# Pace of dispatch scatters, held result scatters and order of first statistics in a gated-recurrence and top-2 MoE kernel

## The chip, the cores and the metric

The kernel runs on one core of a Trainium2 chip. The metric is the device time of one execution in microseconds (us). A core has five engines with in-order queues: PE (matrix multiplication), DVE (vector), ACT (scalar), POOL (GpSimd) and SP (which here only issues DMAs). POOL issues the scatters, that is, indirect DMAs whose rows go to addresses read from a tile.

## The reference, cut to what matters

Input x is 32 sequences of 256 tokens of 128 floats (8192 tokens). For each sequence a modulation from c gives shifts, scales and gates. Then:

```
h   = layernorm(x) * (1 + scale_a) + shift_a
a   = sigmoid(h Wd + bd);  v = h Wv + bv;  g = sigmoid(h Wg + bg)
hs_t = a_t * hs_{t-1} + (1 - a_t) * v_t        (scan over the sequence)
x1  = x + gate_a * hs * g
h2  = layernorm(x1) * (1 + scale_b) + shift_b
p   = softmax(h2 gate_w^T + gate_b) over 8 experts; the two largest are kept
moe = sum over these two of p[e] * (relu(h2 w1[e] + b1[e]) w2[e] + b2[e])
out = x1 + gate_b * moe                        (|gate_a|, |gate_b| at least 0.25)
```

Each expert has w1 of 128x512 and w2 of 512x128, all in fp32.

## The kernel before, in words

**First phase.** The tokens are worked on in 16 supertiles s = 0 to 15 of 512 tokens (T = 4 tiles of 128). A supertile has four steps: `a_norm` (L328: first statistics on DVE by `stats` L292 and `rsqrt` L300, normalised rows xn on ACT), `a_mix` (L349: px transposes, three pz products, the scan on DVE), `a_res` (L385: po transposes, residual, second statistics, rows xm), `a_route` (L401: ph transposes, logits pl, pb transposes, rows `rw` L418, top 2, ranks by the product pq L439, destination rows `pi` L456, and rw's two further columns: weight L461 and the token's result row L462).

**Dispatch.** rw has 8 pieces of 128 rows per supertile. `send` (L472) scatters one by pi into `reg`, a DRAM array that holds the rows of each expert together. The 8 scatters go into the list `sending`; `drip` (L487) takes 1 or 2 of it after each step and gives each a wait on `behind`, an ACT instruction of the step just written: a pace. 128 such scatters run in all.

**Tables and blocks.** After the supertiles of `TAKE` and after the last one, `table` (L497) computes on DVE which blocks of 256 rows of `reg` are full. Blocks 0 to 4 come from supertile 2's table, blocks up to 44 from those up to supertile 12, blocks 45 to 70 from the last. A table's blocks are released when the last scatter of its supertile has been issued.

**Second phase.** A block has four steps: `b_load` (L559, SP: its rows xr and its expert's weights ww; it waits for the latest 16 dispatch scatters), `b_in` (L573: pbx transposes, xs on ACT and DVE), `b_up` (L583: products p, hidden rows hh), `b_down` (L604: products pby, rows yt on ACT, then two result scatters L617 on POOL, yd<-yt). The row index of a result scatter is read from a column of xr. `b_step` (L679) does one step of each of three consecutive blocks and loads four ahead. While the first phase runs, `between` (L710) puts a `b_step` after most of its steps if over two blocks are ready.

**Sums.** `c_base` (L624) adds the experts' biases to xa; `c_load` (L650) reads the two result rows of each token from yd into yk; `c_add` (L660) writes the output. They need constants of `late_constants` (L231), which is called after part 9 of the list of steps.

**What sets the order.** Each engine works in order. The order is that of a list scheduler over the program's own order, with priorities: steps of the first phase from supertile 3 on are moved ahead by `AHEAD`. The first parts are written out in `HEAD` (L31). A tile whose buffers are all in use makes its writer wait: rw has 3 buffers, xr 14, yt 8, yk 3.

Of the kernel before, what the change touches and what calls it, by code (L numbers as in the profile page):

```python
# [8 lines left out]
F32 = mybir.dt.float32  # L9
F32R = mybir.dt.float32r  # L10
BF16 = mybir.dt.bfloat16
I32 = mybir.dt.int32
U32 = mybir.dt.uint32
AF = mybir.ActivationFunctionType
ALU = mybir.AluOpType
AX = mybir.AxisListType
WAIT = mybir.DependencyInfo(mybir.DependencyClass.Sync, mybir.DependencyReason.DATA)

P = 128
# [5 lines left out]
T = 4  # L25
# [4 lines left out]

HEAD = "n0|m0 n1|r0 m1 n2|R0 r1 m2 n3|R1 r2 m3 n4|R2 r3 m4 n5"  # L31

LATE = 9

XE = 3
EARLY = 3
PW = 3
# [3 lines left out]
BACK = 2  # L41
SKIP = 8

HA = 53


YTB = 8
CLAG = 3
HALF = 15

# [4 lines left out]
def adaln_moe(ctx: ExitStack, tc: tile.TileContext, x, Wg, bg, Wv, bv, Wd, bd,  # L55
              gate_w, gate_b, w1, b1, w2, b2, c, wmod, out):
    nc = tc.nc
    NB, S, D = x.shape
    E, _, H = w1.shape
# [3 lines left out]
    NS = N // ST  # L63
    BPS = ST // S
    JB = T // BPS
    K = 2
    CAP = N + BLK
    NJ = BLK // P
    RW = D + 2

    xf = x.rearrange("b s d -> (b s) d")
    of = out.rearrange("b s d -> (b s) d")
# [3 lines left out]
    wk = ctx.enter_context(tc.tile_pool(name="wk", bufs=2))  # L76
    bk = ctx.enter_context(tc.tile_pool(name="bk", bufs=3))
# [18 lines left out]
    xa = cp.tile([P, NS, T, D], F32, name="xa")  # L96
# [7 lines left out]
    rows = cp.tile([P, D], F32, name="rows")  # L104
# [56 lines left out]
    dst = cp.tile([P, NS * T, K], I32, name="dst")  # L161
# [107 lines left out]
    yd = dp.tile([K * N, D], F32, name="yd")  # L269
# [19 lines left out]
    mh = cp.tile([P, T, 1], F32, name="mh")  # L289
    nc.vector.memset(mh, -0.5)  # L290

    def stats(mv, src, name):  # L292
        n = src.shape[1]
        st = wk.tile([P, T, 6], F32, tag=f"st{name[0]}", name=f"st{name}")
        for j in range(n):
            nc.vector.bn_stats(st[:, j], src[:, j])  # L296
        for j in range(n):
            nc.vector.bn_aggr(mv[:, j], st[:, j])

    def rsqrt(mv, name, s):  # L300
# [22 lines left out]
        nc.vector.scalar_tensor_tensor(r, mv[:, :, 0:1], -1.0, y, op0=ALU.mult, op1=ALU.mult)  # L323
        return y, r

    ln1 = {}

    def a_norm(s):  # L328
        g = LN1G.get(s, 0)
        if g:  # L330
            mv = wk.tile([P, g * T, 2], F32, tag=f"mva{g}", name=f"mva{s}")
            for i in range(g):
                stats(mv[:, i * T:(i + 1) * T], xa[:, s + i], f"a{s + i}")
            y, r = rsqrt(mv, f"a{s}", s)
            for i in range(g):
                ln1[s + i] = (y[:, i * T:(i + 1) * T], r[:, i * T:(i + 1) * T])
        y, r = ln1[s]
        xn = wk.tile([P, T, D], F32, tag="xn", name=f"xn{s}")
        for j in range(T):
            last = nc.scalar.activation(xn[:, j], xa[:, s, j], AF.Identity, scale=y[:, j], bias=r[:, j])  # L340
        return dict(s=s, xn=xn, last=last)
# [59 lines left out]
    def a_route(a, base):  # L401
        s, xn = a["s"], a["xn"]
# [50 lines left out]
        pf = wk.tile([P, T, K], F32, tag="pf", name=f"pf{s}")  # L453
        nc.vector.tensor_reduce(pf, op_, axis=AX.X, op=ALU.add)
        pi = wk.tile([P, T * K], I32, tag="pi", name=f"pi{s}", bufs=3)
        nc.vector.tensor_copy(pi, pf.rearrange("p t k -> p (t k)"))  # L456
        sm = wk.tile([P, T], F32, tag="sm", name=f"sm{s}")
        nc.vector.tensor_reduce(sm, e8, axis=AX.X, op=ALU.add)
        rc = wk.tile([P, T], F32, tag="rc", name=f"rc{s}")
        nc.vector.reciprocal(rc, sm)  # L460
        nc.vector.tensor_tensor(rw[:, :, :, D], e8[:, :, 0:K], rc.unsqueeze(2).to_broadcast([P, T, K]), op=ALU.mult)  # L461
        nc.gpsimd.tensor_copy(rw[:, :, :, D + 1].bitcast(I32), dst[:, s * T:(s + 1) * T])  # L462
        nc.vector.tensor_tensor(oh, oh, rw[:, :, :, D].unsqueeze(3).to_broadcast([P, T, K, E]), op=ALU.mult)
        dg = wk.tile([P, T, E], F32, tag="dg", name=f"dg{s}")
        nc.vector.tensor_tensor(dg, oh[:, :, 0], oh[:, :, 1], op=ALU.add)
# [21 lines left out]
    def drip(n, behind):  # L487
        for _ in range(min(n, len(sending))):
            s, send, j, k = sending.pop(0)
            w = send(j, k)  # L490
            tc.add_manual_dep(w, behind.ins.name, WAIT, reason="pace of the rows on their way out")
            sent.append(w)
            if not sending or sending[0][0] != s:
                while held and held[0][0] <= s:
                    blocks.extend(held.pop(0)[1])
# [63 lines left out]
    def b_load(n, tb, i):  # L559
        with tc.issue_after(loaded[-1].ins) if loaded else nullcontext():  # L560
            e = nc.sync.value_load(tb[i:i + 1, 0:1], min_val=0, max_val=E - 1)
            r = nc.sync.value_load(tb[i:i + 1, 1:2], min_val=0, max_val=E * CAP)
        xr = bk.tile([P, NJ, RW], F32, tag="xr", name=f"xr{n}", bufs=YTB + 6)
        w = nc.sync.dma_start(xr, reg[bass.ds(r, BLK)].rearrange("(p t) d -> p t d", p=P))
        tc.add_to_no_dep_group("rows", w.ins)
        for x in sent[-2 * K * T:]:
            tc.add_manual_dep(w.ins, x.name, WAIT, reason="its rows")
        ww = bk.tile([P, WW], F32, tag="ww", name=f"ww{n}", bufs=5)
        b = dict(n=n, xr=xr, ww=ww, tb=tb, i=i)
        loaded.append(nc.sync.dma_start(ww, wd[bass.ds(e, 1)].rearrange("o p f -> p (o f)")))  # L570
        return b

    def b_in(b):  # L573
        n, xr = b["n"], b["xr"]
        px = psb.tile([P, 512], F32, tag="pbx", name=f"pbx{n}")[:, :BLK]
        for j in range(NJ):
            nc.tensor.transpose(px[:, j * P:(j + 1) * P], xr[:, j, 0:D], ident)  # L577
        xs = bk.tile([P, 2, BLK], F32R, tag="xs", name=f"xs{n}")
        nc.scalar.activation(xs[:, 0], px, AF.Copy)  # L579
        nc.vector.tensor_tensor(xs[:, 1], px, xs[:, 0], op=ALU.subtract)  # L580
        b["xs"] = xs

    def b_up(b):  # L583
        n, xs, ww = b["n"], b["xs"], b["ww"]
# [17 lines left out]
        b["hh"] = hh  # L602

    def b_down(b):  # L604
        n, xr, hh, i = b["n"], b["xr"], b["hh"], b["i"]
        py = psb.tile([P, 512], F32, tag="pby", name=f"pby{n}", bufs=2)[:, :NJ * D]
        e = nc.tensor.value_load(b["tb"][i:i + 1, 0:1], min_val=0, max_val=E - 1)
        we = wr[:, bass.ds(e, 1), :].rearrange("p o f -> p (o f)")
        for j in range(NJ):
            for k in range(NH):  # L610
                nc.tensor.matmul(py[:, j * D:(j + 1) * D], hh[:, k, j * P:(j + 1) * P], we[:, k * D:(k + 1) * D],  # L611
                                 start=(j == 0 and k == 0), stop=(j == NJ - 1 and k == NH - 1))
        yt = bk.tile([P, NJ, D], F32, tag="yt", name=f"yt{n}", bufs=YTB)
        for j in range(NJ):
            nc.scalar.activation(yt[:, j], py[:, j * D:(j + 1) * D], AF.Copy, scale=xr[:, j, D:D + 1])  # L615
        for j in range(NJ):
            w = nc.gpsimd.indirect_dma_start(  # L617
                out=yd, out_offset=bass.IndirectOffsetOnAxis(ap=xr[:, j, D + 1:D + 2].bitcast(I32), axis=0),
                in_=yt[:, j], in_offset=None, bounds_check=K * N - 1, oob_is_err=False)
            for g in ("yscat", "yrows"):  # L620
                tc.declare_no_dep(w.ins, group=g, reason="rows of other pairs")
            tc.add_to_no_dep_group("yscat", w.ins)

    def c_base(s):  # L624

# [22 lines left out]
            nc.vector.tensor_tensor(t[:, jq], t[:, jq], g[:, q].unsqueeze(1).to_broadcast([P, JB, D]), op=ALU.mult)  # L648

    def c_load(s):  # L650
        yk = wk.tile([P, K, T, D], F32, tag="yk", name=f"yk{s}", bufs=3)
        step = JB if s >= HALF else T
        for j0 in range(0, T, step):
            for k in range(K):
                r = k * N + s * ST + j0 * P
                w = nc.sync.dma_start(tiles(yk[:, k, j0:j0 + step]), tokens(yd, r, step * P))
                tc.add_to_no_dep_group("yrows", w.ins)
        return s, yk, step
# [20 lines left out]
    def b_step():  # L679

        nonlocal nload
        nonlocal based
        i = len(flow)
        while nload < len(blocks) and nload < i + 1 + LOOK:
            tb, q, ends = blocks[nload]
            blocks[nload] = b_load(nload, tb, q)
            blocks[nload]["ends"] = ends
            nload += 1
        b = blocks[i] if i < len(blocks) else None
        flow.append(b)  # L690
        if b:
            b_in(b)
        if i >= 1 and flow[i - 1]:
            b_up(flow[i - 1])
            drip(1 if alive else 2, flow[i - 1]["last"])
        if i >= 2 and flow[i - 2]:
            b_down(flow[i - 2])
            ended.extend(flow[i - 2]["ends"])
        if not alive and based < NS:
            c_base(based)  # L700
            based += 1
        if len(adding) >= CLAG or (adding and not ended and i >= len(blocks)):
            c_add(*adding.pop(0))
        if ended:
            adding.append(c_load(ended.pop(0)))

    slot = 0
# [2 lines left out]
    def between():  # L710
        nonlocal slot
        slot += 1
        if slot % SKIP and len(blocks) - len(flow) > BACK:
            b_step()

    counts = []
    st = {}
# [16 lines left out]
    for t, todo in enumerate(steps):  # L734
# [37 lines left out]

        for i, s in todo:
            (step0, step1, step2, step3)[i](s)
            drip(2 if t < len(steps) - NS or len(sending) > K * T else 1, st[s]["last"])
            between()
        if t == 0:
            for e in range(E):
                stage(e)
            late()  # L780
        if t == LATE:
            late_constants()
    alive = False
    while len(flow) < len(blocks) + 2 or ended or adding:
        b_step()
    assert not sending and not held


_INS = ['L0_attn_x', 'L0_attn_Wg', 'L0_attn_bg', 'L0_attn_Wv', 'L0_attn_bv', 'L0_attn_Wd', 'L0_attn_bd',
# [25 lines left out]
```

## Time and profile before

| | us |
|---|---|
| median of 12 runs | 468.2 (465.03 to 470.26) |
| the profiled execution | 464.82 |
| its span, first to last instruction | 463.1 |
| busy PE, DVE, ACT, POOL | 380.1, 318.0, 301.2, 293.2 |
| 128 dispatch scatters, L473 | 125.2 busy, 978 ns each |
| 142 result scatters, L617 | 143.3 busy, 1009 ns each |
| block 0 begins (first pbx) | 101.90 |
| block 45 begins | 347.40 |
| block 70 begins | 441.09 |

A line of the timeline reads: start, length, engine, line of the kernel, operation, out<-in by the program's names, how many, and in brackets the idle time of that engine just before with what ended it. "issue" is idle time for which the profile shows no wait. In the slices the span is cut into 40 parts of 11.6 us; each digit is an engine's busy share in tenths. In the table of windows each engine's busy us is followed by its number of instructions.

### The profile page before, as it was taken

How to read it: one execution, taken by the hardware profiler on the slowest of the kernel's cores; microseconds unless marked ns; L12 is line 12 of the kernel's file. 1: busy time of each engine (PE TensorE's matmuls, PEld its weight loads, DVE VectorE, ACT ScalarE, POOL GpSimd, SP SyncE). 2: the span in 40 equal slices, each digit the busy share in tenths (PEclk: the TensorE clock that was granted, in tenths of full speed). 3: DMA queues.
4: the chain of work that ended last, by engine and by line, in shares of the span. 5: the costliest groups of instructions: out<-in, count | busy, mean ns of one | idle time of the engine just before them, and what ended most of it. 6: DMA issues, size and time to landing. Idle time of an engine off the chain costs nothing.

```text
span 463.1 us, 11442 instructions
## 1 busy us (share of the span) xinstructions
PE 380.1 (82%) x2803; PEld 332.9 (72%) x2803; DVE 318.0 (69%) x1638; ACT 301.2 (65%) x742; POOL 293.2 (63%) x322
## 2 busy tenths in 40 slices
PE   3827467659999999996899869999838999989980
PEld 3315243438898899895898859899837999889980
DVE  7997999979889888784579634766425320464484
ACT  3857366577986998893687635767524667667750
POOL 4633655354777777777777777777774555546651
PEclk9975777778999999999799988999996999999996
DMA  6996211037736484555563765887429977999994
GB/s 199 366 339 213 83 35 35 29 102 243 224 112 185 150 234 151 170 164 168 167 181 97 226 188 154 236 245 206 121 65 282 280 236 239 303 342 332 325 341 142
DMA packets 55413, 91.57 MB, mean 198 GB/s; under 512 B 8654, under 2 KB 39964, under 8 KB 55350
## 3 DMA queue, kind: packets, MB, share of 16 engines
q1 hardware_dynamic: 46624, 73.89, 53.0%
q0 software_dynamic: 8672, 16.94, 10.5%
q8 instruction: 25, 0.41, 0.4%
q14 instruction: 38, 0.31, 0.2%
q10 hardware_dynamic: 54, 0.02, 0.0%
HBM read 64.30 MB, written 27.43 MB: 198 GB/s over the span
## 4 chain that ended last, share of the span: by engine, by line
PE 50%; DMA 21%; DVE 13%; issue 6%; ACT 5%; POOL 4%; SPq 1%; POOLq 0%; ACTq 0%; DVEq 0%
PE pby L611 18%; PE pz L362 7%; DMA yd<-yt,xr 7%; DMA reg<-rw,pi 6%; PE p L592 5%; PE p L593 5%; PE p L594 5%; DMA yk<-yd 4%; PE pbx L577 3%; DMA ww<-wd 2%; DMA xr<-reg 2%; POOL reg L473 2%; DVE sta L296 2%; PE px L353 2%; PE po L390 1%
## 5 line engine op out<-in xcount | busy, mean ns | idle before, releaser
L617 POOL DMA_INDIRECT yd<-yt,xr x142 | 143.3, 1009 | 72.9 <-ACT yt L615 32.4
L473 POOL DMA_INDIRECT reg<-rw,pi x128 | 125.2, 978 | 61.5 <-issue 23.8
L611 PE MATMUL pby<-wr,hh 128*128 x1136 | 160.8, 279 | 0.6 <-ACT hh L600 0.5
L611 PEld LDWEIGHTS pby<-wr,hh 128*128 128x128 f32 x1136 | 145.3, 194 | 6.7 <-issue 4.1
L600 ACT ACTIVATE hh<-p,ww 128x256 f32<-128x256 f32 x231 | 98.9, 474 | 33.7 <-PE p L594 25.4
L592 PE MATMUL p<-xs,ww 128*128 128x256 f32 x284 | 91.1, 322 | 0.4 <-issue 0.4
L593 PE MATMUL p<-xs,ww 128*128 128x256 f32 x284 | 81.1, 286 | 0.0
L594 PE MATMUL p<-xs,ww 128*128 128x256 f32 x284 | 81.0, 285 | 0.0
L615 ACT ACTIVATE yt<-pby,xr 128x128 f32<-128x128 f32 x142 | 44.6, 369 | 25.5 <-PE pby L611 25.4
L362 PE MATMUL pz<-h,wT 128*128 128x512 f32 x96 | 56.6, 710 | 5.4 <-ACT tg L377 2.9
L592 PEld LDWEIGHTS p<-xs,ww 128*128 128x128 f32 x284 | 54.7, 193 | 2.4 <-issue 1.9
L593 PEld LDWEIGHTS p<-xs,ww 128*128 128x128 f32 x284 | 55.0, 194 | 0.5 <-issue 0.5
L594 PEld LDWEIGHTS p<-xs,ww 128*128 128x128 f32 x284 | 54.6, 192 | 0.0
L580 DVE TENSOR_TENSOR xs<-pbx,xs 128x256 fp32r<-128x256 f32 x71 | 29.6, 417 | 25.6 <-ACT xs L579 25.6
L577 PE MATMUL pbx<-ident,xr 128*128 128x128 f32 x142 | 28.6, 283 | 14.9 <-DMA xr<-reg 12.8
L362 PEld LDWEIGHTS pz<-h,wT 128*128 128x128 f32 x96 | 19.6, 233 | 24.7 <-issue 11.3
L579 ACT ACTIVATE xs<-pbx 128x256 fp32r<-128x256 f32 x71 | 27.8, 392 | 13.4 <-PE pbx L577 13.3
L598 DVE TENSOR_SCALAR hh<-p,ww 128x256 f32<-128x256 f32 x53 | 25.4, 479 | 15.2 <-ACT hh L600 14.8
L340 ACT ACTIVATE xn<-xa,nra,nya 128x128 f32<-128x128 f32 x64 | 26.5, 494 | 10.9 <-DVE nra L323 10.9
L398 ACT ACTIVATE xm<-xa,nrb,nyb 128x128 f32<-128x128 f32 x64 | 26.5, 484 | 10.1 <-DVE nrb L323 10.0
L665 DVE TENSOR_TENSOR ot<-yk 128x512 f32<-128x512 f32 (+1 forms) x17 | 11.2, 660 | 30.9 <-DMA yk<-yd 30.1
L418 ACT ACTIVATE rw<-pb 128x1024 f32<-128x1024 f32 x16 | 16.4, 1025 | 23.8 <-DMA reg<-rw,pi 19.9
(191 smaller groups left out, 636.0 us busy)
## 6 DMA issues: line engine op xcount, KB each, us to landing
ww<-wd SPq DMA_DIRECT2D x71, 514.0 KB
xr<-reg SPq DMA_DIRECT2D x71, 130.0 KB
yk<-yd SPq DMA_DIRECT2D x30, 256.0 KB
wd<-wh SPq DMA_DIRECT2D x8, 514.0 KB
xa<-in_L_attn_x_dram SPq DMA_DIRECT2D x16, 256.0 KB
out_dram<-ot SPq DMA_DIRECT2D x15, 256.0 KB
yd<-yt,xr POOLq DMA_INDIRECT x142
w1s<-in_L_ffn_w_dram SPq DMA_DIRECT2D x8, 256.0 KB
```

The lines of the kernel that those rows point to most:

```text
L362: nc.tensor.matmul(z, wT[:, i], h1, start=True, stop=True)
L473: w = nc.gpsimd.indirect_dma_start(out=reg, out_offset=bass.IndirectOffsetOnAxis(ap=pi[:, j * K + k:j * K + k + 1], axis=0), in_=rw[:, j, ...
L577: nc.tensor.transpose(px[:, j * P:(j + 1) * P], xr[:, j, 0:D], ident)
L579: nc.scalar.activation(xs[:, 0], px, AF.Copy)
L580: nc.vector.tensor_tensor(xs[:, 1], px, xs[:, 0], op=ALU.subtract)
L592: nc.tensor.matmul(z, hi, xs[:, 0], start=True, stop=False)
L593: nc.tensor.matmul(z, hi, xs[:, 1], start=False, stop=False)
L594: nc.tensor.matmul(z, lo, xs[:, 0], start=False, stop=True)
L600: w = nc.scalar.activation(hh[:, k], p1[:, k - k0], AF.Relu, bias=bias)
L611: nc.tensor.matmul(py[:, j * D:(j + 1) * D], hh[:, k, j * P:(j + 1) * P], we[:, k * D:(k + 1) * D], start=(j == 0 and k == 0), stop=(j == ...
L615: nc.scalar.activation(yt[:, j], py[:, j * D:(j + 1) * D], AF.Copy, scale=xr[:, j, D:D + 1])
L617: w = nc.gpsimd.indirect_dma_start(out=yd, out_offset=bass.IndirectOffsetOnAxis(ap=xr[:, j, D + 1:D + 2].bitcast(I32), axis=0), in_=yt[:, ...
```

## The change

1. **Results wait.** `b_down` no longer issues its two result scatters; it puts them in the list `results`. `results_out`, called by `b_step`, issues them, oldest first and ordered behind the latest dispatch scatter. While dispatch goes on it leaves up to 8 blocks' scatters in the list (up to block 8 all, from there fewer, none from about block 24 to 28, then again up to 8); afterwards it issues 3 per block, and all before a `c_load`. For this yt has 16 buffers, xr 9 instead of 14, and a DVE copy keeps each block's row indices in a tile of its own, xi. yk takes the buffers of rw.
2. **No pace at first.** `drip` gives the scatters of supertiles 0 to 2 no wait, and issues all 8 after the routing step. Later, once the first phase is written, it takes 3 per block instead of 2. `between` starts with the step given by `FIRST`.
3. **First statistics stay back.** The `bn_stats` of `a_norm` are ordered, without a wait, behind the pi of the supertile routed last in the program's order.
4. The copy of `dst` into rw moves from POOL to DVE.
5. `late_constants` is called after all steps.

```
-LATE = 9
+FIRST = (6, 1)
-YTB = 8
+HOLD0 = 28
+HOLD = 8
+XRB = 9
+YTB = 8 + HOLD
...
-            nc.vector.bn_stats(st[:, j], src[:, j])
+            w = nc.vector.bn_stats(st[:, j], src[:, j])
+            if behind:
+                tc.add_manual_dep(w.ins, behind.name, ORDER, reason="not ahead of the supertiles that route")
...
-                stats(mv[:, i * T:(i + 1) * T], xa[:, s + i], f"a{s + i}")
+                stats(mv[:, i * T:(i + 1) * T], xa[:, s + i], f"a{s + i}", placed[-1] if placed else None)
...
-        nc.gpsimd.tensor_copy(rw[:, :, :, D + 1].bitcast(I32), dst[:, s * T:(s + 1) * T])
+        nc.vector.tensor_copy(rw[:, :, :, D + 1].bitcast(I32), dst[:, s * T:(s + 1) * T])
...
-            tc.add_manual_dep(w, behind.ins.name, WAIT, reason="pace of the rows on their way out")
+            if s >= EARLY:
+                tc.add_manual_dep(w, behind.ins.name, WAIT, reason="pace of the rows on their way out")
...
-        xr = bk.tile([P, NJ, RW], F32, tag="xr", name=f"xr{n}", bufs=YTB + 6)
+        xr = bk.tile([P, NJ, RW], F32, tag="xr", name=f"xr{n}", bufs=XRB)
...
+        xi = bk.tile([P, NJ], I32, tag="xi", name=f"xi{n}", bufs=YTB + 3)
+        nc.vector.tensor_copy(xi, xr[:, :, D + 1].bitcast(I32))
+        b["xi"] = xi
...
-        for j in range(NJ):
+        def send(j):
             w = nc.gpsimd.indirect_dma_start(
-                out=yd, out_offset=bass.IndirectOffsetOnAxis(ap=xr[:, j, D + 1:D + 2].bitcast(I32), axis=0),
+                out=yd, out_offset=bass.IndirectOffsetOnAxis(ap=xi[:, j:j + 1], axis=0),
                 in_=yt[:, j], in_offset=None, bounds_check=K * N - 1, oob_is_err=False)
...
+        results.extend((send, j) for j in range(NJ))
+    results = []
+    def results_out(most, left=0):
+        for _ in range(min(most, len(results) - left)):
+            send, j = results.pop(0)
+            with tc.issue_after(sent[-1]):
+                send(j)
...
-        yk = wk.tile([P, K, T, D], F32, tag="yk", name=f"yk{s}", bufs=3)
+        yk = wk.tile([P, T, K, RW], F32, tag="rw", name=f"yk{s}", bufs=3)
+        yk = yk.rearrange("p t k r -> p (t k r)")[:, :K * T * D].rearrange("p (k t d) -> p k t d", k=K, t=T)
...
-            drip(1 if alive else 2, flow[i - 1]["last"])
+            drip(1 if alive else 3, flow[i - 1]["last"])
...
+        if alive or sending:
+            results_out(K * T, NJ * min(max(HOLD - max(i - HOLD, 0) // 2, i - HOLD0, 0), HOLD))
+        else:
+            results_out(NJ + 1)
...
         if ended:
+            results_out(len(results))
             adding.append(c_load(ended.pop(0)))
...
-            drip(2 if t < len(steps) - NS or len(sending) > K * T else 1, st[s]["last"])
-            between()
+            drip(K * T if i == 3 and s < EARLY else 2 if t < len(steps) - NS or len(sending) > K * T else 1, st[s]["last"])
+            if (t, i) >= FIRST:
+                between()
...
-        if t == LATE:
-            late_constants()
+    late_constants()
```

More of the change, by code (lines that the diff above doesn't have):

```diff
@@ L16 @@
 AX = mybir.AxisListType
+ORDER = mybir.DependencyInfo(mybir.DependencyClass.NoSync, mybir.DependencyReason.DATA)
 WAIT = mybir.DependencyInfo(mybir.DependencyClass.Sync, mybir.DependencyReason.DATA)
@@ L290, in adaln_moe, with stats @@
     nc.vector.memset(mh, -0.5)
-    def stats(mv, src, name):
+    def stats(mv, src, name, behind=None):
         n = src.shape[1]
@@ L324, in rsqrt @@
         return y, r
+    placed = []
     ln1 = {}
@@ L455, in a_route @@
         pi = wk.tile([P, T * K], I32, tag="pi", name=f"pi{s}", bufs=3)
-        nc.vector.tensor_copy(pi, pf.rearrange("p t k -> p (t k)"))
+        placed.append(nc.vector.tensor_copy(pi, pf.rearrange("p t k -> p (t k)")).ins)
         sm = wk.tile([P, T], F32, tag="sm", name=f"sm{s}")
@@ L604, in b_down @@
     def b_down(b):
-        n, xr, hh, i = b["n"], b["xr"], b["hh"], b["i"]
+        n, xr, hh, i, xi = b["n"], b["xr"], b["hh"], b["i"], b["xi"]
         py = psb.tile([P, 512], F32, tag="pby", name=f"pby{n}", bufs=2)[:, :NJ * D]
@@ L785, in adaln_moe @@
         b_step()
-    assert not sending and not held
+    assert not sending and not held and not results
 _INS = ['L0_attn_x', 'L0_attn_Wg', 'L0_attn_bg', 'L0_attn_Wv', 'L0_attn_bv', 'L0_attn_Wd', 'L0_attn_bd',
```

## Prediction

> **What bounds the kernel now.** I read four views in this order: the page's slices (which engine is full when), the chain that ended last, a table of busy time by stage (columns: window, its length, then busy us with counts for PE, PEld, DVE, ACT, POOL, then the granted clock, DMA share and GB/s), and single instructions at the seams.
>
> ```profile
> PE   3827467659999999996899869999838999989980
> DVE  7997999979889888784579634766425320464484
> POOL 4633655354777777777777777777774555546651
> ```
> ```profile
> PE 50%; DMA 21%; DVE 13%; issue 6%; ACT 5%; POOL 4%; SPq 1%; POOLq 0%; ACTq 0%; DVEq 0%
> PE pby L611 18%; PE pz L362 7%; DMA yd<-yt,xr 7%; DMA reg<-rw,pi 6%; PE p L592 5%; PE p L593 5%; PE p L594 5%; DMA yk<-yd 4%; PE pbx L577 3%; DMA ww<-wd 2%; DMA xr<-reg 2%; POOL reg L473 2%; DVE sta L296 2%; PE px L353 2%; PE po L390 1%
> ```
> PE is full from slice 10 on, except in slices 18 to 28 here and there and at slice 29; up to slice 9 it is half idle while DVE is full. Half the chain is PE, but 13% of it are the two kinds of scatter, which POOL issues.
>
> ```profile
> 45.00:102.00 57.00, 35.11 (x136) 19.44 (x135) 53.90 (x369) 32.54 (x69) 31.96 (x34) 0.77 0.15 48
> 102.00:120.00 18.00, 17.16 (x125) 14.58 (x126) 14.88 (x105) 14.22 (x36) 8.16 (x11) 0.87 0.75 219
> 120.00:200.00 80.00, 79.53 (x630) 71.58 (x630) 69.10 (x394) 69.12 (x177) 61.99 (x66) 1.00 0.60 182
> 200.00:288.00 88.00, 75.76 (x592) 69.84 (x592) 55.95 (x321) 56.36 (x143) 67.86 (x73) 0.92 0.57 165
> 330.00:352.00 22.00, 12.81 (x93) 11.13 (x94) 8.23 (x21) 7.33 (x18) 16.82 (x18) 0.86 0.41 126
> ```
> ```profile
> 101.90 0.69 PE L577 MATMUL pbx<-ident,xr 128*128 128x128 f32 x2 [2.45 <-DMA xr<-reg]
> ...
> 347.40 0.69 PE L577 MATMUL pbx<-ident,xr 128*128 128x128 f32 x2 [7.01 <-DMA xr<-reg]
> ```
> The first is block 0, the second block 45, the first that needs the last table. Block 44 began at 330.09; blocks there are 3.9 us apart, so 347.40 − 330.09 − 3.9 = **13.4 us** of the span are a stall. It ends 3.5 us after POOL's last dispatch scatter:
>
> ```profile
> 74.23 0.96 POOL L473 DMA_INDIRECT reg<-rw,pi  x1 [3.12 <-ACT xn L340]
> ...
> 86.66 0.97 POOL L473 DMA_INDIRECT reg<-rw,pi  x1 [3.08 <-ACT rw L418]
> ...
> 94.16 0.96 POOL L473 DMA_INDIRECT reg<-rw,pi  x1 [5.27 <-ACT xm L398]
> ...
> 342.95 0.96 POOL L473 DMA_INDIRECT reg<-rw,pi  x1 [0.30 <-DMA yd<-yt,xr]
> ```
> The upper three are scatters of supertiles 0 to 2 that wait for the pace, not for data: such waits spread 24 of them over 45 to 95 us, and block 0 needs the 24th, the one at 94.16.
>
> So I split the span at three pbx starts: **stage 1** to block 0, 101.9; **stage 2** to block 36 (297.4), 195.5; **stage 3** to block 70 (441.1), 143.7; **end** 22.0; together 463.1. Around the span lie 1.7 us (464.8 for that execution), and the median of the runs, 468.2, lies 3.4 above it.
>
> **Part 1, no pace for the first 24 scatters, first statistics held back.** A scatter takes 0.96 us and the next follows 0.30 later, 1.27 together. Supertile 1's destinations (pi) are written at 58.96, supertile 2's at 67.95. Ahead of these DVE also did first statistics (64 × 277 + 64 × 153 ns, with the chain behind them 2.2 us a supertile) of some eight supertiles, 17 us, that no block needs yet. They go behind. Of it I take 2 us as gain for supertile 1's pi, because the path to pi runs through ACT and PE as well; bounds 0 and 8. From there POOL issues 16 scatters one behind the other (supertile 2's pi is there before the ninth), 16 × 1.27 = 20.3; 2.8 for landing and 2.2 for the load, as of the first blocks before: 58.96 − 2 + 20.3 + 5 = **82 us** (76 to 90; the upper end if supertile 2's nyb, a POOL operation that now stands behind supertile 0's eight scatters and two weight operations of 1.27, comes late by 8). Gain 20 in stage 1.
>
> Most of it is work that only moves. In the order of PE's instructions block 0 now stands 2.5 px, 2 pz, 2 po, 2 ph/pl/pb and 1 pq groups earlier. At the 120–200 rates (per supertile px 0.6, pz 2.9, po 0.6, ph, pl and pb 2.2, pq 0.4) that is 1.6 + 5.8 + 1.3 + 4.4 + 0.4 = 13.4 us more PE in stage 2. PE's work there was 17.16 + 79.53 + 75.76 and 8.5 up to block 36: 181.0 in 195.5 us, a share of 92.6%. Now 194.4; at that share **210 us**. Below: PE never waiting, 197. Above: DVE. It had 146.5; to it come nine supertiles' statistics, 20, some 1.75 supertiles of routing and mixing at 11.8 (the lines L292 to L471 had 59 us in 120–200, for five supertiles), 20.7, the copies of part 3, 7.5: 195. At the 86% that DVE reached in 120–200 these take 226. I take 210: PE's own share already holds 12 us idle in 200–288, and DVE would stand at 93%, as in 45–102 (53.9 of 57).
>
> **Part 2, results wait.** Up to 16 result scatters stay behind dispatch scatters. In POOL's order the last dispatch scatter is the 190th instead of the 210th. POOL runs without pause from 117 us on, with 41 done there, 169 more in 226.5 us, 1.34 each. After: 40 are due by about 115 too (24 without pace, two supertiles); so the 190th ends near 343 − 20 × 1.3 = 317, and block 45 can start at 320.5. PE reaches block 45 at 82 + 210 + 32.7 (block 36 to 44 before) + 3.9 = 328.6. The stall is gone with 8 us to spare: **stage 3** 143.7 − 13.4 = 130.3. If POOL is later by more than 8 us, each further one costs one. The held scatters come later, at 3 per block, where POOL is half idle (46.68 busy of 89 us in 352–441); so I cost them at nothing, and at most 8 × 1.3 = 10 if they reached the end.
>
> **Part 3, copies.** 71 int copies of 128×2 on DVE; nearest row the 128×8 cast L456, 209 ns, small chain operations 155: I take 0.15 each, 36 in stage 2, 5.4; 12 of the 16 dst copies 2 us (POOL's 243 ns are their price there); both in the sum of part 1. In stage 3 DVE is at 40%, nothing. The xr buffers fall from 14 to 9; with four blocks loaded ahead and three in work eight are in use: nothing, at most a load's 2.2 us at a few blocks.
>
> These DVE copies also meet POOL's descriptor work. Scatters beside DVE work took 0.96 in the middle, 1.36 at most. The Trainium skill, "SBUF — State Buffer", section "SBUF: two separate sides", says that DVE and GpSimd share a port pair which one instruction holds alone, and that an fp32 copy inside SBUF on VectorE keeps GpSimd from writing descriptors. By that rule 87 more copies could cost POOL an estimated 87 × 0.15 = 13 us, which would eat the margin and give 454 in place of 449. The trace shows scatters near their minimum among hundreds of DVE instructions, so I don't add it.
>
> **Part 4, late constants.** Thirteen small DVE operations (3.2 us, 135 to 141 before), eight loads on SP and a POOL memset (0.5) go to the last routing; on SP the loads keep their place in the order, so nothing is queued behind them that was not before. DVE is freer there (26 of 42 us in 288–330): nothing, at most 3.2. yk in rw's buffers: first needed when dispatch is over: nothing.
>
> **Sum.** 82 + 210 + 130.3 + 22 = 444.3, with 1.7 around it 446.0 against 464.8, −18.8; against the median 468.2 that is **449**.
>
> **Rivals.**
> *DVE bounds stage 2.* For: 195 us of work, and its order is fixed with the xi copies ahead of earlier blocks' work. Against: DVE ran at 95% in 45–102. At 226: 82 + 226 + 130.3 + 22 + 1.7 + 3.4 = 465; I give it 458 to 468.
> *Slower: the xi copy of a table's first block stops DVE.* In DVE's order the copy of block 29 stands right behind supertile 11's pi, that of 37 behind supertile 14's, that of 45 behind 15's and ahead of block 44's xs. Each waits for a load that waits for the last scatter of supertile 10, 12 or 15; routing, xs and hh stand behind it. In the new order supertile 10's last is the 134th scatter: 60 by 133 us and 74 × 1.34 later, 232; DVE comes there at 215 to 221. So 11 to 17 us; some of that is the idle time already in PE's share (ACT waited 6.55 and 6.66 for buffers of the same scatters). It decides from 19 us beyond it, over 6 a place; at 12 a place 36 − 19 = 17 over: 485.
> *No gain.* The 20 us of stage 1 are given back (PE idles in stage 2 as long, the last dispatch scatter is as late): 466 to 470.
> *More.* Both full engines without loss and block 0 at 76: 76 + 197 + 130.3 + 22 + 5.1 = 430.
>
> **How the numbers follow.** Forecast (440 to 458) 0.55, DVE 0.18, slower 0.12, no gain 0.08, more 0.07. Under 0.5%, 2.3 us, this kernel's runs can't tell from no change: faster (below 465.9) 0.55 + 0.07 + two thirds of DVE's, 0.12, = 0.74; same 0.08 + 0.06 = 0.14; slower 0.12. The range leaves out the slower case, half of "more" and the top of "no gain": 435 to 468.
>
> **What would show it.** Block 0's pbx at 76 to 90, and supertiles 0 to 2's scatters 1.27 apart from their pi on; if it starts later, the pace was not what held them. Block 36 near 292 with PE at 92% between; DVE over 95% there, or DVE idle before xi waiting for xr, names the first two rivals. Last dispatch scatter near 317, and pbx of block 45 without a wait of several us for xr. Scatters still near 0.97 us. The prediction fails if stage 2 takes over 225 us.

## The result and the profile after

The changed kernel takes 488.2 us (median of 15 runs, 484.69 to 490.53), the kernel before 467.9 (62 runs): ratio **1.0435**, 95% interval 1.0416 to 1.0454. Its profiled execution took 489.51 us, its span is 487.8. By the four stages of the prediction, in us:

| | before | forecast | after |
|---|---|---|---|
| stage 1, to block 0 | 101.9 | 82 | 81.7 |
| stage 2, to block 36 | 195.5 | 210 | 239.2 |
| stage 3, to block 70 | 143.7 | 130.3 | 144.5 |
| end | 22.0 | 22 | 22.5 |

Block 0 starts where it was forecast. All of the miss is in stages 2 (+29) and 3 (+14). PE is busy 206.2 of the 239.2 us of stage 2 (86%); the forecast had 194.4 of 210 (92.6%). The slices of the changed kernel (12.2 us each now):

```profile
PE   4754662997698799889888796998989999699980
DVE  7868893789886698756774676676746631445584
POOL 3737653015514577777777777457777777466561
```
PE is below 9 in most slices from 10 to 27, where before it was near 9. POOL shows 0, 1, 5, 5, 1 from slice 7 on, then 7s. A scatter is busy 0.97 us and the next starts 0.30 later, so **7 is a full POOL**: 0.97 of 1.27.

Next the table of windows, first of the kernel before, then of the changed one (POOL is the fifth busy time with its number of instructions). The bounds are events: a stretch begins or ends with the last dispatch scatter of supertile 5 (149 and 153) or 11 (263 and 294); 77 is that of supertile 2 in the changed kernel, and 117.40 is the first result scatter of the kernel before.

```profile
117.40:149.00 31.60, 31.60 (x254) 28.63 (x254) 28.72 (x166) 26.40 (x68) 24.43 (x26) 1.00 0.56 171
149.00:263.00 114.00, 105.89 (x829) 96.15 (x828) 85.79 (x478) 88.43 (x223) 88.06 (x95) 0.97 0.58 169
```
```profile
77.00:103.60 26.60, 20.18 (x133) 17.41 (x134) 13.98 (x74) 17.70 (x43) 0.96 (x1) 0.75 0.42 130
103.60:153.00 49.40, 39.52 (x239) 30.39 (x239) 43.63 (x327) 33.32 (x77) 22.81 (x24) 0.83 0.32 98
153.00:294.00 141.00, 124.73 (x914) 109.76 (x914) 98.29 (x603) 97.03 (x242) 101.99 (x102) 0.96 0.53 157
```
Before, POOL issues 88 scatters (48 of dispatch, 40 of results) in the 114 us between supertiles 5 and 11: 88 × 1.30 = 114, and between two of its instructions there is no gap above the usual 0.30. So POOL is full in this stretch, while PE is busy 105.89 of the 114 us. After, 24 scatters leave in the 49.4 us before 153, where there was room for 38, and none of them is a result. The results held there come out behind: 48 + 54 in the next 141 us (12 fewer results than before ahead of this stretch, 14 more in it, 22 fewer between it and the last dispatch scatter: 62 instead of 82 in all). The last dispatch scatter starts at 354.78 instead of 342.95.

The gap after supertile 2's scatters, and block 5, in the timeline of the changed kernel:

```profile
101.22 0.18 PE L448 MATMUL pq<-mk,tri 128*128 128x40 bf16 x1
...
103.62 0.96 POOL L482 DMA_INDIRECT reg<-rw,pi  x1 [25.44 <-ACT hh L614]
...
132.53 0.69 PE L587 MATMUL pbx<-ident,xr 128*128 128x128 f32 x2 [2.93 <-DMA xr<-reg]
```
Blocks 0 to 4 now stand ahead of supertile 3 on PE, so its rank product comes at 101.22 (89.66 before), POOL idles for 25 us, and block 5 waits until 132.53. A later pause of POOL shows where the held-back statistics act:

```profile
152.65 0.96 POOL L482 DMA_INDIRECT reg<-rw,pi  x1 [0.30 <-ACT hh L614]
158.76 1.26 ACT L349 ACTIVATE xn<-xa,nra,nya 128x128 f32<-128x128 f32 x3 [2.82 <-DVE nra L330]
160.95 0.95 POOL L482 DMA_INDIRECT reg<-rw,pi  x1 [7.34 <-ACT xn L349]
```
The scatter at 160.95 is the first of supertile 6, whose pi is written at 147.78. It waits for its pace, an xn of a later supertile, and that xn waits for nra, the end of a chain that begins with first statistics at 147.86, right behind that pi.

Two more stalls are new, in stage 3, both on SP's in-order queue:

```profile
328.00 7.34 SPq L563 DMA_DIRECT2D reg<-pad  x7
...
336.99 0.35 SPq L574 DMA_DIRECT2D xr<-reg  x1
...
340.46 0.44 PE L587 MATMUL pbx<-ident,xr 128*128 128x128 f32 x2 [1.93 <-DMA xr<-reg]
```
```profile
414.72 0.93 SPq L684 DMA_DIRECT2D yk<-yd  x2
416.99 0.36 SPq L574 DMA_DIRECT2D xr<-reg  x1
418.51 0.69 DVE L693 TENSOR_TENSOR ot<-yk 128x512 f32<-128x512 f32 x1 [8.09 <-DMA yk<-yd]
...
419.59 0.69 PE L587 MATMUL pbx<-ident,xr 128*128 128x128 f32 x2 [4.17 <-DVE xs L590]
```
First block 39, 12.0 us after block 38: its load stands behind the pad writes of the last table. Before, such writes (292.60 to 301.03) held a load back as well, to 301.87, but PE had blocks enough and began one every 4 us. Then a yk load that waits 6.2 us for result scatters, with the loads of the next blocks behind it on SP: block 58 begins 8.0 us after block 57, where 3.4 is usual there. The stall ahead of block 45 did shrink as forecast: 366.33 − 359.00 = 7.3 us after block 44, without a wait for xr, instead of 17.3. So in stage 3 the shorter stall and the new ones cancel: 144.5 us against 143.7.

### The profile page after: what moved, and what is told of

Same layout as the page of the kernel before. It is cut to its first block, busy times and chain, and to the rows that moved or that the text cites. A ratio compares the mean times of both kernels' runs of the same rounds, so it can differ in the third digit from the quotient of the medians.

```text
span 487.8 us, 11431 instructions
## 1 busy us (share of the span) xinstructions
PE 393.7 (81%) x2803; PEld 341.3 (70%) x2803; DVE 323.4 (66%) x1725; ACT 303.4 (62%) x742; POOL 293.5 (60%) x306
## 4 chain that ended last, share of the span: by engine, by line
PE 27%; DMA 23%; DVE 10%; issue 10%; POOL 6%; ACT 5%; SPq 4%; POOLq 1%; ACTq 0%; DVEq 0%
PE pby L625 11%; DMA reg<-rw,pi 8%; DMA xr<-reg 7%; POOL reg L482 4%; PE p L606 4%; PE p L607 3%; PE p L608 3%; DMA yd<-yt,xi 2%; DMA yk<-yd 2%; DMA ww<-wd 2%; PE pbx L587 2%; POOL yd L632 2%; PE pz L371 1%; ACT xn L349 1%; ACT xm L407 1%
## 5 line engine op out<-in xcount | busy, mean ns | idle before, releaser
L632 POOL DMA_INDIRECT yd<-yt,xi x142 | 146.2, 1030 | 58.8 <-issue 22.2
L606 PE MATMUL p<-xs,ww 128*128 128x256 f32 x284 | 94.0, 333 | 4.6 <-DMA ww<-wd 2.0
L607 PE MATMUL p<-xs,ww 128*128 128x256 f32 x284 | 83.4, 294 | 0.0
L608 PE MATMUL p<-xs,ww 128*128 128x256 f32 x284 | 82.6, 291 | 0.0
L594 DVE COPY xi<-xr 128x2 int32<-128x2 int32 x71 | 14.3, 202 | 87.9 <-DMA xr<-reg 85.1
L606 PEld LDWEIGHTS p<-xs,ww 128*128 128x128 f32 x284 | 56.6, 200 | 9.6 <-DVE hh L612 2.7
L371 PE MATMUL pz<-h,wT 128*128 128x512 f32 x96 | 60.2, 749 | 3.2 <-ACT h L366 1.1
L607 PEld LDWEIGHTS p<-xs,ww 128*128 128x128 f32 x284 | 57.2, 201 | 0.7 <-issue 0.7
L608 PEld LDWEIGHTS p<-xs,ww 128*128 128x128 f32 x284 | 56.7, 200 | 0.1
L587 PE MATMUL pbx<-ident,xr 128*128 128x128 f32 x142 | 29.6, 292 | 22.2 <-DVE xs L590 11.8
L587 PEld LDWEIGHTS pbx<-ident,xr 128*128 128x128 f32 x142 | 17.5, 147 | 27.4 <-DVE xs L590 13.4
L371 PEld LDWEIGHTS pz<-h,wT 128*128 128x128 f32 x96 | 20.7, 246 | 20.5 <-issue 12.9
```

The source lines that it names most:

```text
L371: nc.tensor.matmul(z, wT[:, i], h1, start=True, stop=True)
L606: nc.tensor.matmul(z, hi, xs[:, 0], start=True, stop=False)
L607: nc.tensor.matmul(z, hi, xs[:, 1], start=False, stop=False)
L608: nc.tensor.matmul(z, lo, xs[:, 0], start=False, stop=True)
L632: w = nc.gpsimd.indirect_dma_start(out=yd, out_offset=bass.IndirectOffsetOnAxis(ap=xi[:, j:j + 1], axis=0), in_=yt[:, j], in_offset=None, ...
```

## The experiments

**Theory T**, formed after the first eight runs: two parts of the change each slow the same stretch, supertiles 5 to 11, so undoing one shows little. *Hold*: results held while POOL had room are drained where it is full. *Loop*: first statistics of supertile s+3 (later s+4 and s+5) behind the pi of s make a closed loop, routing, statistics, norm, mix, res, routing, whose latency sets the period. **Rivals:** A, the xi copies that stop DVE; B, the early blocks; C, the late statistics (C1 through the loop, C2 because they do not fit in the block phase at all); D, the dst copy on DVE; H, the hold alone.

The runs, as ratio to the kernel before in the same call (on the first chips 467 to 469 us; e9 to e18 ran on two chips on which it took 536 to 541, where only ratios of one call are compared; see the last section):

| run | us | ratio (interval) |
|---|---|---|
| e1 change, xi behind xs | 485.1 | 1.034 (1.027 to 1.042) |
| e2 change, pace kept | 493.1 | 1.053 (1.046 to 1.059) |
| e3 change, statistics free | 479.7 | 1.028 (1.021 to 1.034) |
| e4 before, only pace away | 466.5 | 0.998 (0.994 to 1.002) |
| e5 change, no hold | 487.4 | 1.036 (1.030 to 1.042) |
| e6 change, dst copy on POOL | 491.4 | 1.050 (1.043 to 1.056) |
| e7 before, only hold | 478.2 | 1.019 (1.015 to 1.024) |
| e8 before, only statistics behind pi | 481.9 | 1.028 (1.023 to 1.033) |
| e9 as e7, xi behind xs | 553.8 | 1.029 (1.023 to 1.035) |
| e10 as e9, no hold | 536.9 | 1.001 (0.997 to 1.005) |
| e11, e18 before, statistics three pi older | 533.6, 542.3 | 0.993 (0.989 to 0.997), 1.000 (0.995 to 1.004) |
| e12, e16 change, xi, statistics, dst undone | 564.6, 569.0 | 1.054 (1.047 to 1.060), 1.060 (1.051 to 1.070) |
| e13, e17 change, no hold, statistics free | 540.7, 546.5 | 1.008 (1.004 to 1.012), 1.009 (1.005 to 1.013) |
| e14 as e12, hold from block 28 on | 558.0 | 1.038 (1.028 to 1.048) |
| e15 as e10, hold from block 28 on | 542.8 | 1.012 (1.004 to 1.020) |

**Round 1.**
```
e1  +        tc.add_manual_dep(xi copy, xs copy, ORDER)
e2  -            if s >= EARLY:                      and 2 per step again
e3  -  stats(..., placed[-1] if placed else None)    +  stats(..., None)
e4  before  +            if s >= EARLY:              and 8 at once after routing
```


> The changed kernel with one edit: each xi copy is ordered on DVE behind its own block's xs, so it never stands ahead of a load; everything else of the order is nearly unchanged. Theory A (in the changed kernel DVE stops 53 times, 85.1 us in all, at xi copies whose xr is not loaded, and the work behind them makes stage 2 long): the xi waits go, stage 2 falls from 239 to some 210, time 455 to 468. Theory B (blocks 0 to 4, now ahead of supertile 3 on PE, delay every later supertile by some 10 us and leave a gap of 31 us before block 5; the xi waits are only where that lateness shows): 482 to 490, pbx of block 5 still near 132.

> The changed kernel with the pace of supertiles 0 to 2 put back (wait and 2 per step as before). Theory B: block 0 returns to about 100 us, supertile 3's pi to about 93, no gap after block 4, time 462 to 472. Theory A: the xi copies still stand ahead of the loads, DVE still waits for xr some 60 to 90 us, time 480 to 495.

> The changed kernel without the order of the first statistics behind pi. Theory C (held-back statistics make ACT wait for nra, 20.4 us over 9 times, and PE for xn, 33 us, in the block phase where DVE is full): 470 to 480. Theories A and B: the statistics are work that only moves; 483 to 492, and block 0 a few us later.

> The kernel before with only the pace of supertiles 0 to 2 taken away (no wait, 8 at once after routing); no xi copy, results sent at once, first statistics as before. Theory A: a gain of 5 to 20, 448 to 463, since nothing stops DVE. Theory B: blocks 0 to 4 ahead of supertile 3 delay the rest, 470 to 485, with a gap before block 5.

The waits of the changed kernel, then of e1 (us in total, times, longest):
```profile
DVE xi L594 <- DMA xr<-reg: 85.1, 53, 5.0
```
```profile
DVE xs L590 <- ACT xs L589: 28.3, 16, 6.2
DVE rw L471 <- DMA reg<-rw,pi: 15.8, 4, 7.5
```
In e1 the 85.1 us are gone, and the time falls by 3 (by ratio from 1.043 to 1.034). Rival A is refuted as the main cause: DVE now waits elsewhere, for the blocks' ACT copies and for buffers of rw. e3 fits rival C of its expectation, but its 479.7 leave 12 us of the loss. e1 lies in the range of rival B, but B falls too: the pace put back makes it slower (e2), and the pace taken away alone changes nothing (e4), although block 0 starts at 84 there. Supertile 3's product comes at 101 in e4, the last dispatch scatter of supertile 5 at 153 (149 before), and from there POOL is full in both; block 36 still begins 4 us earlier than before (293.15), but the last dispatch scatter comes 4 us later (346.64), and block 45, which waits for it, begins at 351.13 (347.40 before).

**Round 2.**
```
e5  -  results_out(K * T, NJ * min(max(HOLD - ...), HOLD))   +  results_out(K * T)
e6  -  nc.vector.tensor_copy(rw[..., D + 1], dst)            +  nc.gpsimd.tensor_copy(...)
e7  change with pace, free statistics, dst copy on POOL, FIRST (0, 0), constants after part 9
e8  before  +  stats(..., placed[-1] if placed else None)
```


> The changed kernel with no result scatter held while dispatch goes on (each is issued with its block, as before). Theory H (the held scatters come out in the dispatch of supertiles 7 to 11, 55 of them, so that the buffers of rw come free late and routing with them): 466 to 475. If the loss lies in DVE's order (statistics, dst copy, xi): 483 to 492.

> The changed kernel with the dst copy back on POOL. Theory D (on DVE that copy stands ahead of the one-hot and rank work and waits for a buffer of rw, that is for scatters of the supertile three before, so routing waits: 15.8 us in four waits in the run with xi behind xs): 474 to 482. Otherwise 484 to 491.

> The changed kernel with everything but the held results undone: pace back, first statistics free, dst copy on POOL, constants after part 9, blocks from the first step on. It keeps the list of results, the xi copies as they stand, 9 xr and 16 yt buffers, 3 scatters per block afterwards. Theory H: 478 to 490, most of the loss. If the statistics and the dst copy carry it: 462 to 472.

> The kernel before with only the first statistics ordered behind pi. Theory C (late statistics; the run of the changed kernel without that order was 8.5 us faster): 474 to 480. If they cost only together with the early blocks: 465 to 471.

Hold alone costs 8.8 us, the order of the statistics alone 12.5: together 21, the size of the whole loss. But without the hold the change stays nearly as slow (e5), and e6 refutes D. e7 lies at the lower edge of H's range, e8 2 us above C's. The stretch in numbers (the rank products and scatters of the traces, us; "hold" and "statistics" mark which of the two the run has, "after" has both):

| | rank product, period of s = 5 to 11 | dispatch of s = 6 to 11 | scatters × 1.30 |
|---|---|---|---|
| before | 16.3 | 114 | 88, 114 |
| e4 | 15.7 | 112 | 86, 112 |
| after | 20.8 | 141 | 102, 133 |
| e7 hold | 18.5 | 134 | 100, 130 |
| e3 hold | 19.0 | 139 | 100, 130 |
| e8 statistics | 19.0 | 122 | 90, 117 |
| e5 statistics | 20.7 | 125 | 88, 114 |

With the hold POOL has 100 to 102 scatters there, 10 to 16 more than without, and little room: beyond the usual gaps it is idle for 3 us in e7, 8 in the changed kernel and 10 in e3. With the statistics alone (e5, e8) it is idle for 11 and 4 us, and routing itself comes every 21 and 19 us.

The same traces by the stages of the prediction, in us (the traced execution of the kernel before is 3 us faster than its median, so differences to it are too large by as much):

| | stage 1 | stage 2 | stage 3 |
|---|---|---|---|
| before | 101.9 | 195.5 | 143.7 |
| e4, no pace | 83.5 | 209.6 | 149.7 |
| e7, hold, with the pace | 99.5 | 211.6 | 142.9 |
| e3, hold, no pace | 84.9 | 226.3 | 143.2 |
| e8, statistics, with the pace | 114.4 | 196.6 | 143.7 |
| e5, statistics, no pace | 81.2 | 241.7 | 143.2 |
| after, both, no pace | 81.7 | 239.2 | 144.5 |

The hold costs 16 us in stage 2, with the pace (e7 against before) and without it (e3 against e4, where other parts of the change differ too). The statistics are another matter. In e8 block 0 comes 12.5 us late, as much as the whole loss, and stage 2 is only 1 us longer than before; there the paced scatters of supertiles 0 to 2 wait longer, and the 24th leaves at 104.74 instead of 94.16, although supertile 2's pi is written at 70.18:

```profile
102.97 1.47 POOL L477 DMA_INDIRECT reg<-rw,pi  x1 [6.93 <-DVE ntb L319]
```
In the changed kernel, which has no pace there, block 0 is not late; the order of the statistics costs in stage 2 instead (13 us between e3 and the changed kernel), and there undoing the hold alone shortens nothing (e5). So the sum 8.8 + 12.5 has the size of the loss by chance. And the longer period of routing alone does not prove the loop: e8 has it too without a longer stage 2. A rival stands beside the loop, that scatters from supertile 3 on, which are still paced, wait for ACT work behind the late statistics, as at 160.95 above. No run has the order without any pace, so the two are not told apart.

**Round 3, and repeats.**
```
e9   e7 with e1's edit          e10  e9 with e5's edit
e11, e18  e8 with  placed[-3] if len(placed) > 2 else None
e12, e16  change with the edits of e1, e3, e6
e13, e17  change with the edits of e3, e5
e14  e12 with   results_out(K * T, NJ * min(max(i - HOLD0, 0), HOLD))     e15  e9 with it
```


> The kernel of the run with only the held results, with each xi copy ordered on DVE behind its own block's xs. If the xi waits (82.0 us there, 52 times) are what cost 8.8 us: 464 to 471. If the hold itself, the 9 xr buffers or the later scatters cost it: 475 to 480.

> As the run before it, but no scatter is held while dispatch goes on; xi copies behind xs, 9 xr and 16 yt buffers and 3 scatters per block at the end stay. If the hold itself delays or helps, this run differs from the one before it: a help of the hold (20 scatters fewer ahead of the last dispatch scatter) would make this one 5 to 13 us slower; a harm would make it 5 to 10 faster. If neither, both within 2 us.

> The kernel before with the first statistics ordered behind the pi three routed supertiles further back. Theory C1 (ordered behind the newest pi, the statistics of supertile s+3 close a loop: routing of s, statistics, then norm, mix, res and route of s+3, and this latency sets the period): 467 to 471, the 12.5 us of the run with the newest pi gone. Theory C2 (statistics do not belong in the block phase at all, because DVE is full there): 476 to 483.

> The changed kernel with three parts undone that put DVE work in the way: xi copies behind xs, first statistics free, dst copy on POOL. Held results and the early scatters without pace stay. If these three carry the loss: 455 to 468, block 0 near 84 and block 45 without the 13 us stall. If the early blocks and the hold carry part: 470 to 478.

> The changed kernel with two parts undone: no result scatter held while dispatch goes on, and first statistics free. xi copies ahead of loads, dst copy on DVE and early scatters without pace stay. Theory T (two limits of the same stretch, each enough alone: held scatters drained into the dispatch of supertiles 6 to 11, and statistics closed into a loop with routing; so undoing one gave 1 and 8.5 us and undoing both gives nearly all): 464 to 471. If the xi waits or the dst copy are a third limit: 474 to 482.

> As the run with three DVE parts undone (xi behind xs, statistics free, dst copy on POOL), but scatters are held only from block 28 on, so none is drained into supertiles 6 to 11. Theory T: dispatch of supertiles 6 to 11 takes about 114 us as before instead of 141, the last dispatch scatter comes 10 to 20 us earlier than 343, the stall ahead of block 45 shrinks: 450 to 463. If holding as such is harmful: 470 or more.

> The kernel before with the list of results, xi copies behind xs and the hold from block 28 on only, pace kept. Theory T: 455 to 466, faster than before by most of its 13.4 us stall. If the gain of fewer scatters ahead of the last dispatch is hidden otherwise: 466 to 470.

> The kernel of the run with three DVE parts undone once more, on a chip on which the kernel before runs at its usual time. Theory T: the drain of held scatters alone limits supertiles 6 to 11: 473 to 482. If the three DVE parts carried the loss: 455 to 468.

> The changed kernel with no scatter held while dispatch goes on and first statistics free, once more, on a chip on which the kernel before runs at its usual time (on the other it stood 0.8% above the kernel before). Theory T: 466 to 473, against 479.7 with the hold and 487.4 with the statistics' order. If xi waits or the dst copy limit as well: 474 to 482.

> The kernel before with first statistics behind the pi three routed supertiles further back, once more (0.7% below the kernel before on the other chip; behind the newest pi it was 2.8% above on the usual one). Theory C1 (a closed loop costs, not the place in the block phase): 463 to 470. Theory C2: 476 to 483.

All ran on the two slower chips, so their times answer to no expectation in us; the ratios do. e9 and e10 differ in the hold alone: 1.029 against 1.001. So neither the list, the nine xr buffers nor xi copies behind xs cost anything there; the hold does. e11 and e18: ordered behind an older pi the same statistics cost nothing, although up to 200 us into the run they still stand among the blocks, so C2 fails there. It also fits the loop; but e8 itself was not run on these chips. e13 and e17: with hold and order both undone 0.8 to 0.9% are left, by ratio at the upper edge of theory T's ranges, against 5.4 to 6.0% for the change with the hold and without the three DVE parts (e12, e16). Those two lie above every range that was expected for them (by ratio, at most 1.03). e14 and e15: a hold from block 28 on drains nothing into supertiles 6 to 11 (40 results there, as before), and still is 1.2% slower alone and 3.8% in the change without the three DVE parts. My expectation of a gain failed. Against e11, on the other of the two chips, e15's last dispatch scatter does come earlier, at 384 instead of 399 us, and block 36 at 342 instead of 347; then blocks 36 to 44 take 72 us instead of 51, with ACT waits of up to 13 us whose releaser the trace does not name (timelines of e15, then of e9):
```profile
381.34 0.84 ACT L615 ACTIVATE hh<-p,ww 128x256 f32<-128x256 f32 x2 [9.48 <-remote]
...
411.04 0.62 ACT L630 ACTIVATE yt<-pby,xr 128x128 f32<-128x128 f32 x2 [13.25 <-remote]
```
```profile
426.70 0.62 ACT L630 ACTIVATE yt<-pby,xr 128x128 f32<-128x128 f32 x2 [16.09 <-remote]
```
The same stretch is where the hold costs in the other runs of these chips. Blocks 36 to 44 take 71 to 75 us in e9, e12, e15 and e16, and 51 to 56 in e10, e11, e13, e14, e17 and e18 (in e14, which also holds, block 45 comes 20 us after block 44 instead); on the first chips they take 36 us with the hold alone (e7) and 33 before. Block 36 itself begins in e9 only 3 us later than in e10, and in e16 only 2 us later than in e13. And POOL is not full in supertiles 6 to 11 there: beyond the usual gaps it is idle for 31 to 34 us in e9, e10 and e11. So these chips confirm that the hold costs, but not theory T's reason for it, which rests on e7 and the counts of the first chips. What releases the waits is open. No version tried is faster than the kernel before by more than a measurement tells (the 0.7% of e11 did not come again in e18).

## Why the prediction was wrong

- **The step that failed: stage 2 = 194.4 / 0.926 = 210.** This takes PE's work at PE's old share and has no term for results that are drained while POOL is full, nor for anything that waits behind the late statistics. Stage 2 took 239.2, with PE busy 206.2. For the early start alone the step held: stage 2 of e4 is 209.6. The hold by itself adds 16 (e7, and e3 against e4), the order of the statistics 13 more (e3 against the changed kernel). The two do not simply add: without the hold, in e5, stage 2 is no shorter (241.7).
- **Part 2, the hold**: it was credited with 20 scatters fewer ahead of the last dispatch scatter, 26 us, and its held scatters were to come out where POOL is half idle. But the hold is already drained between blocks 8 and 24: in supertiles 6 to 11 leave 54 results instead of 40, where POOL was full before. The count of 20 fewer was right, but 12 of them were taken out of time ahead of that stretch, in which POOL has idle time.
- **Part 2, "40 are due by about 115 too … near 317"**: by 115 us 28 had begun, and the 40th left at 131, because blocks 0 to 4 delayed supertile 3. The other 150 took 1.49 us each, 28 us of it idle time beyond the usual gaps, so 317 became 355. The count of the kernel before was off too: by 117.4 us 36 scatters had begun, not 41, and the other 174 take 1.30 us each, not 1.34.
- **What bounds the kernel now**: half right. Part 2 saw that POOL runs without pause from 117 us on, but the bounds of stage 2 were taken from PE and DVE alone; POOL entered only as a date for block 45. Counted, 88 scatters at 1.30 us fill the 114 us between supertiles 5 and 11.
- **Part 1, block 0 at 82**: right in the number, 81.67, but partly by luck. Supertile 1's pi came at 53.65 (56.96 in the sum), supertile 2's only at 66.91, after the scatters of supertile 1 were out, so that POOL stood 3.7 us; block 0 began 3.5 us after the end of the 24th scatter, where 5 were counted. e4 has the early start alone and gains nothing, since about 40 scatters have begun by 123 us with or without the pace, and from there POOL pauses 3 us in all up to the last dispatch scatter.
- **Part 1, "work that only moves"**: wrong for the statistics. I priced them as 2.2 us of DVE a supertile; what counted was what they stand behind. Behind the newest pi they cost 12.5 us alone (e8, all ahead of block 0) and 8.5 in the change (e3); behind older ones nothing on the slower chips (e11, e18).
- **Part 2, the held scatters at the end cost nothing**: wrong by some 5 us ahead of block 58, where a yk load waits for result scatters on SP, the next blocks' loads behind it; the bound of 10 held.
- **Part 3, copies**: cost near the forecast; xi took 169 ns in the middle and the waits before them, 85.1 us, were worth 3 us (e1). By the rule of the Trainium skill ("SBUF — State Buffer", section "SBUF: two separate sides") I estimated 13 us for POOL. The scatters' means rose from 1009 to 1030 and from 978 to 987 ns: 142 × 0.021 + 128 × 0.009 = 4 us at most.
- **Part 4**: no run shows a cost; the late constants alone were not tried.
- **Rivals**: the time of the slower rival, 485, was nearly hit, but its mechanism was not what decided: of its three places only waits of up to 5.0 us are in the trace, and without them the kernel takes 485.1.

Left open: how the 20 us divide on the first chips with both parts undone (e13 and e17 ran on the others), and what the last 0.9% there is (xi ahead of loads, dst copy, constants, the first block step, or the early blocks). How the order of the statistics makes stage 2 longer, by the loop or by the pace of the scatters, is argued and not shown by a run of its own; so is why e12 loses more than e9.

## What to carry to other kernels

Before you move work of an engine, count its instructions in the stretch times their full spacing, gap included: an engine that shows 70% busy can be full. Work held back from idle time into a full stretch can cost its whole length there (12 scatters at 1.30 against 16 us in e7), even if fewer instructions stand ahead of the one you want early. An order without a wait still costs what then waits behind it; ask what stands behind the newest result of a pipeline, and try an older one.

## What was not expected of the hardware

The same 2803 PE instructions took 393.7 us busy instead of 380.1, while the granted clock fell from 0.914 to 0.893 on average, and the p products of the first line went from 322 to 333 ns. PE's idle time alone does not explain the clock: in 45 to 102 us PE is busy 35.1 us in both kernels, and the clock is 0.77 before and 0.66 after. No run separates the cause.

On the two chips of e9 to e18 the kernel before took some 15% more. In the waits of e11 engines stand for several us with a releaser that the trace calls remote, another core or an unknown queue:
```profile
DVE rk L453 <- remote: 24.6, 4, 8.5
ACT hh L604 <- remote: 19.4, 5, 5.4
```
Its scatters take the same 987 and 1008 ns, so it is not the length of POOL's scatters. The cause was not looked into, and no trace of the kernel before was kept from these chips.
